# Block matching before a convolution stack: a pair of offsets in one subtraction and one square

## The chip, the core and the metric

The kernel runs on one core of a Trainium2 chip. The metric is the device time of one execution in microseconds. The profile comes from one profiled execution of the same program; "the span" is its time from first to last instruction. The engines are PE (TensorE, with its weight loads shown apart as PEld), DVE (VectorE), ACT (ScalarE), POOL (GpSimd) and SP (SyncE). Each runs its own list of instructions in order and waits on semaphores for the others.

## The reference

`x` is 8 images of 32 channels, 128 x 128, float32. It passes two layers, each with a group norm in front and a residual sum behind. The first layer begins with a block matching, and that is what the change is about:

```python
for dy in range(-SEARCH_R, SEARCH_R + 1):          # SEARCH_R = 2: 25 offsets
    for dx in range(-SEARCH_R, SEARCH_R + 1):
        yy = jnp.clip(jnp.arange(Hn) + dy, 0, Hn - 1)
        xx = jnp.clip(jnp.arange(Wn) + dx, 0, Wn - 1)
        sh = x[:, :, yy][:, :, :, xx]
        d = ((x - sh) ** 2).sum(1, keepdims=True)
        costs.append(_conv(d, ones, pad=PATCH // 2))   # 3x3 sum
...
_, idx = jax.lax.top_k(-jnp.transpose(cost, (0, 2, 3, 1)), K)   # K = 8
...
h = jax.nn.relu(_conv(_conv(xb, w1), w2, groups=CK, pad=1))
h = jax.nn.relu(_conv(_conv(h, w3), w4, groups=CK, pad=1))
wiener = jax.nn.sigmoid(_conv(_conv(h, w5), w6, groups=CK, pad=1))
filt = _conv(wiener * dct, inv_dct_w, groups=C)
```

For every pixel the 8 offsets of least cost are taken, the 8 shifted copies of the image are gathered into 256 channels (`xb`), and these pass three pointwise and three 3x3 depthwise convolutions and a filter. The second layer is a 5x5 convolution of each channel.

## The kernel before

**Layout of the block matching.** A normalised image stands in the tile `xn`: 128 partitions are 4 groups of rows by 32 channels, and each partition holds 38 rows of 132 columns (`HR`, `HX`): 32 rows of its own with 3 above and 3 below, and 128 columns with 2 of border on each side, filled with copies of the edge. A shift by an offset is then only another start address in the same tile. Since the squared difference for an offset and that for its opposite are the same numbers shifted, only 12 of the 25 offsets are computed (numbers 13 to 24; 12 is zero).

**Squares.** `prep(b)` (L364) normalises image `b` (L382, one operation on DVE) and then walks over 6 blocks of 6 rows (`SR`), and in each over 6 pairs of offsets: 36 pairs an image, 288 in all. A pair is one task, `squares` (L431), in three steps. On DVE, two subtractions (L442), one for each offset, of 6 rows and as many columns as the offset leaves: 132 for dx = 0, 131 for |dx| = 1, 130 for |dx| = 2, so 792, 786 or 780 elements a partition. On ACT, two squares (L450) in place. On PE, matmuls (L457) with a column of minus ones that add up the 32 channels and put each offset's cost in a row of its own of the PSUM tile `pd`; there are 2 by 2 of them in the code and 8 matmul instructions a pair in the trace. After the sixth pair `pd` is copied (L468) and sent to DRAM (L472), from where `costs` (L483) reads it back, sums 3x3 on DVE, transposes on PE and finds the 8 best with `max` and `max_index` (L534, L535). `places` (L540) turns these into addresses for the gather of the next image.

The difference tile `df` has the tag "df" and 4 buffers, each of 6 x 132 float32 a partition, so two pairs are in flight. A fifth subtraction waits for the matmuls that read the first.

**Order.** The instructions of PE, DVE and ACT stand in an order that the program writes out by hand. The main loop takes steps of 8 rows; in each step it goes through the three convolution stages of three different row blocks and the final filter of a fourth. Beside it run tasks in four queues: "D" (DVE work, run by `tick` for a credit, where a pair costs `PAIR` = 1.95 and at most two are taken in one round), "A" (ACT), "P" and "Q" (PE). A task gives up at each `yield` and is put into the queue that the yield names. In one stage of a step the order is about this: PE's pointwise matmuls for 128 of the 256 channels (L671) and their copies on ACT (L679); ACT's first tap of the depthwise convolution (L722); queue "P", then queue "Q" with the matmuls of the squares; a selector pass on ACT for the gather (L617, L618); `tick`, and with it the subtractions on DVE; the other eight taps of the depthwise convolution on DVE (L725, 8 x 1024 elements); pointwise matmuls for the other 128 channels (L695, copies L702); gather matmuls (L632, copy L639); queue "A" with the squares; the function of the previous depthwise stage (L729) on ACT; another selector pass; and the depthwise matmuls (L751, copies L764).

So on DVE the subtractions stand in front of the eight accumulates of L725, and on ACT the squares stand behind a selector pass and the copies, and in front of L729. The squares of image `b + 1` are computed while image `b` is convolved, mostly in the first two fifths of its time; those of image 0 come before everything else. One image takes some 812 us.

Of the kernel before, what the change touches and what calls it, by code (L numbers as in the profile page):

```python
# [8 lines left out]
F32 = mybir.dt.float32  # L9
BF16 = mybir.dt.bfloat16  # L10
U32 = mybir.dt.uint32
AF = mybir.ActivationFunctionType
# [3 lines left out]
P = 128  # L16
C, K, H, W = 32, 8, 128, 128
# [9 lines left out]
HX = W + 4  # L27
SR = 6
# [15 lines left out]
def bm3d_conv_preact(  # L44
# [16 lines left out]
    nc = tc.nc  # L61
# [5 lines left out]
    work = ctx.enter_context(tc.tile_pool(name="work", bufs=2))  # L67
# [142 lines left out]
    def push(task):  # L210
        want = next(task, None)
        if want:
            which, cost, *wait = want
            queues[which].append((cost, task, now[0] + (wait[0] if wait else 0)))
# [149 lines left out]
    def prep(b):  # L364
# [25 lines left out]
        for i in range((HR - 2) // SR):  # L390
            pd = ps_d.tile([P, SR // 2, HX], F32, name=f"pd_{b}_{i}", tag="pd")

            for aa in ((2, 4), (0, 0), (1, 1), (3, 2), (4, 3), (5, 5)):
                yield "D", PAIR
                push(squares(b, i, pd, xn, aa, sq, idx))
# [35 lines left out]
    def squares(b, i, pd, xn, aa, sq, idx):  # L431


        r0 = SR * i
        ds = []
        for e in range(2):
            o = 13 + 2 * aa[e] + e
            dy, dx = o // 5 - 2, o % 5 - 2

            ca, cz = max(0, -dx), min(HX, HX - dx)  # L440
            df = work.tile([P, SR, HX], F32, name=f"df_{b}_{i}_{o}", tag="df", bufs=4)
            nc.vector.tensor_sub(  # L442
                df[:, :, ca:cz],
                xn[:, r0 : r0 + SR, ca:cz],
                xn[:, r0 + dy : r0 + dy + SR, ca + dx : cz + dx],
            )
            ds.append((df, ca, cz))
        yield "A", 0
        for df, ca, cz in ds:
            nc.scalar.activation(df[:, :, ca:cz], df[:, :, ca:cz], AF.Square)  # L450
        yield "Q", 0

        for e in range(2):
            for h in range(2):
                df, ca, cz = ds[e]
                j = 2 * e + h
                nc.tensor.matmul(  # L457
                    pd[C * j : C * (j + 1), :, ca:cz],
                    neg[:, 28 - 4 * aa[e] : 60 - 4 * aa[e]],
                    df[:, SR // 2 * h : SR // 2 * (h + 1), ca:cz],  # L460
                    start=aa[0] == 2,
                    stop=aa[0] == 5,
                    skip_group_check=True,
                )
        if aa[0] < 5:
            return
        sm = work.tile([P, SR // 2, HX], F32, name=f"sm_{b}_{i}", tag="sm", bufs=1)
        nc.scalar.copy(sm, pd)  # L468
        for e in range(2):
            for h in range(2):  # L470
                j = 2 * e + h
                nc.gpsimd.dma_start(  # L472
                    sq[e::2, :, r0 + SR // 2 * h : r0 + SR // 2 * (h + 1)].rearrange(
                        "o g r x -> o g (r x)"
                    ),
                    sm[C * j : C * j + 24].rearrange("p r x -> p (r x)"),
                )

        q = {1: 0, 3: 1, 4: 2, 5: 3}.get(i)
        if q is not None:  # L480
            push(costs(b, q, sq, idx))
# [553 lines left out]
    with tc.manual_schedule(engines=ORDERED):  # L1035
# [19 lines left out]
        for s in range(len(steps) + 2):  # L1055
            if s < len(steps):
                b, n = steps[s]
# [120 lines left out]
```

## Time and profile before

Three runs: 6686.44, 6694.62 and 6697.99 us, median 6694.62. The profiled execution took 6691.29 us, with a span of 6689.5 us and a mean granted clock of 0.976.

| group | count | busy us | mean ns |
|---|---|---|---|
| DVE accumulate L725 | 3264 | 4032.5 | 1237 |
| PE depthwise matmuls L751 | 31680 | 2142.4 | 422 |
| ACT selector L617 | 1024 | 1170.9 | 1143 |
| ACT selector L618 | 1024 | 1086.1 | 1061 |
| PE matmuls of the squares L457 | 2304 | - | 518 to 534 |

Busy time is the time in which at least one instruction of the group ran; instructions of one engine overlap a little at their ends, so the busy time of a group is less than its count times the mean. "Idle before" is time in which the engine stood still just in front of an instruction, and the releaser is what ended that wait. The chain of waits is followed back from the last instruction; in this profile it reaches from 3509 us to the end.

Who waits in and around the squares, from the rows of their three lines: ACT for the subtractions 341.1 us in 87 waits (316.3 us in 70 waits after the first image's squares); DVE's subtractions for a free buffer 78.4 us in 18 waits; PE's matmuls for the squares 204.0 us in 255 waits (115.1 us in 168 after the first image's).

### The profile page before, as it was taken

The numbers are of one execution on the slowest core, as the hardware profiler recorded it, in microseconds if no ns is written. First come the engines' busy times: TensorE is split into PE (matmuls) and PEld (weight loads), VectorE is DVE, ScalarE is ACT, GpSimd is POOL, SyncE is SP. The second block draws the span as 40 slices with busy tenths as digits, with TensorE's granted clock in tenths as the row PEclk, the third lists the DMA queues.
The fourth block names the chain that finished last, engine by engine and source line by source line (L and its number), as shares of the span: only waits on it lengthen the run. The fifth ranks groups of instructions, "written<-read, shape, count | busy, mean of one in ns | idle before, by whom it ended". The sixth has DMA issues, their size and how long they took to land. (4 is left out here: it accounts for less than half of the span.)

```text
span 6689.5 us, 235037 instructions
## 1 busy us (share of the span) xinstructions
PE 6258.1 (94%) x102306; PEld 3229.6 (48%) x102306; DVE 5864.5 (88%) x8826; ACT 5055.3 (76%) x6698; POOL 3536.2 (53%) x5527
## 2 busy tenths in 40 slices
PE   4899899999999999999999999999999999999997
PEld 1444455544545445554454444544445454554553
DVE  7899988999889998899889988899988999877786
ACT  5787778777787777877787776877768777687772
POOL 8365447554475454754546544565446654445334
PEclk8899999999999999999999999999999999999998
DMA  4666666766566675666756657566665666566663
GB/s 95 150 153 153 151 151 151 173 153 158 150 165 157 159 161 137 162 162 156 172 138 164 161 142 168 144 167 158 152 154 151 167 155 154 142 170 163 154 155 80
DMA packets 811718, 1021.56 MB, mean 153 GB/s; under 512 B 257072, under 2 KB 622192, under 8 KB 810688
## 3 DMA queue, kind: packets, MB, share of 16 engines
q0 software_dynamic: 424608, 747.17, 43.9%
q1 hardware_dynamic: 383568, 258.11, 17.8%
q8 instruction: 805, 13.19, 0.8%
q10 hardware_dynamic: 2512, 1.25, 0.1%
q14 instruction: 225, 1.84, 0.1%
HBM read 554.82 MB, written 217.54 MB: 115 GB/s over the span
## 5 line engine op out<-in xcount | busy, mean ns | idle before, releaser
L725 DVE SCALAR_TENSOR_TENSOR acc<-tv,dwv,acc 128x1024 f32<-128x1024 f32 (+3 forms) x3264 | 4032.5, 1237 | 247.6 <-ACT acc L722 143.0
L751 PE MATMUL pw<-t,dwd 128*32 128x254 f32 (+7 forms) x31680 | 2142.4, 422 | 81.4 <-DMA t<-t 61.3
L603 POOL DMA_DIRECT2D ib<-idxd x1024 | 749.9, 733 | 1586.3 <-ACT sel L618 1311.6
L751 PEld LDWEIGHTS pw<-t,dwd 96*32 96x32 f32 (+1 forms) x31680 | 1090.4, 111 | 921.0 <-issue 445.7
L617 ACT ACTIVATE ib<-ib,nplace 128x1024 bf16<-128x1024 bf16 x1024 | 1170.9, 1143 | 49.5 <-DMA ib<-idxd 49.5
L618 ACT ACTIVATE sel<-ib 128x1024 f32<-128x1024 bf16 x1024 | 1086.1, 1061 | 32.5
L695 PE MATMUL p<-acc,lw 128*32 128x256 f32 x16768 | 1001.6, 383 | 23.7 <-ACT tv L679 23.0
L671 PE MATMUL pv<-acc,lw 128*32 128x512 f32 x8448 | 956.3, 590 | 46.5 <-DVE acc L818 39.8
L791 POOL DMA_DIRECT2D xf<-xbd x1088 | 651.3, 627 | 267.8 <-DMA out_dram<-xy 80.7
L695 PEld LDWEIGHTS p<-acc,lw 128*32 128x32 f32 x16768 | 575.0, 111 | 439.0 <-issue 82.5
L450 ACT ACTIVATE df<-df 128x786 f32<-128x786 f32 (+2 forms) x576 | 468.2, 861 | 343.7 <-DVE df L442 341.1
L679 ACT COPY tv<-pv 128x512 f32<-128x512 f32 (+2 forms) x784 | 437.5, 579 | 320.3 <-PE pv L671 309.4
L632 PE MATMUL pg<-sel,xt 120*32 120x88 f32 (+1 forms) x24576 | 616.0, 244 | 62.8 <-ACT sel L618 48.2
L632 PEld LDWEIGHTS pg<-sel,xt 120*32 120x32 f32 x24576 | 556.7, 111 | 235.6 <-ACT sel L618 71.0
L442 DVE TENSOR_TENSOR df<-xn 128x786 f32<-128x786 f32 (+2 forms) x576 | 531.7, 973 | 79.4 <-PE pd L457 78.4
L729 ACT ACTIVATE acc<-acc 128x1024 f32<-128x1024 f32 (+3 forms) x408 | 417.3, 1023 | 241.0 <-DVE acc L725 240.8
L764 ACT ACTIVATE acc<-pw 128x512 f32<-128x512 f32 (+2 forms) x808 | 438.7, 572 | 194.1 <-PE pw L751 192.9
L671 PEld LDWEIGHTS pv<-acc,lw 128*32 128x32 f32 x8448 | 281.4, 111 | 537.8 <-issue 435.2
L702 ACT COPY t<-p 128x512 f32<-128x512 f32 x800 | 424.3, 571 | 116.0 <-PE p L695 115.5
L722 ACT ACTIVATE acc<-tv,dwv 128x1024 f32<-128x1024 f32 (+3 forms) x408 | 455.1, 1115 | 36.5 <-PE pa L831 22.9
L671 PE MATMUL pv<-xb,lw 128*32 128x512 f32 x4096 | 470.9, 594 | 0.0
L695 PE MATMUL p<-xb,lw 128*32 128x256 f32 x8192 | 467.7, 379 | 0.0
(155 smaller groups left out, 5936.0 us busy)
## 6 DMA issues: line engine op xcount, KB each, us to landing
ib<-idxd POOLq DMA_DIRECT2D x1024, 256.0 KB, 4.6
xbd<-xb POOLq DMA_DIRECT2D x128, 1024.0 KB, 7.0
xf<-xbd POOLq DMA_DIRECT2D x960, 128.0 KB, 7.2
t<-t SPq DMA_DIRECT2D x792, 128.0 KB
t<-t SPq DMA_DIRECT2D x384, 256.0 KB
tv<-tv SPq DMA_DIRECT2D x384, 130.0 KB
xt<-xtd POOLq DMA_DIRECT2D x240, 180.0 KB, 4.6
xtd<-xl POOLq DMA_DIRECT2D x192, 96.0 KB, 3.1
```

The lines of the kernel that those rows point to most:

```text
L442: nc.vector.tensor_sub(df[:, :, ca:cz], xn[:, r0 : r0 + SR, ca:cz], xn[:, r0 + dy : r0 + dy + SR, ca + dx : cz + dx],)
L450: nc.scalar.activation(df[:, :, ca:cz], df[:, :, ca:cz], AF.Square)
L603: nc.gpsimd.dma_start(ib.rearrange("p g k y x -> p g (k y x)"), idxd[b][s4 % 8 // 2, s4 // 8 * 2 + s4 % 2, f] .rearrange("(g e k) x -> e g ...
L617: nc.scalar.activation(ib, ib, AF.Square, bias=nplace)
L618: nc.scalar.activation(sel, ib, AF.Relu, scale=-1.0, bias=1.0)
L632: nc.tensor.matmul(pg[C * j : C * (j + 1), :, :, xa:xz], xt[: 8 * QW, f * (NT // 2) + t], sels[j // 2][: 8 * QW, :, j % 2, :, xa:xz], star ...
L671: nc.tensor.matmul(ps[C * j : C * (j + 1), :hr], lhsT[:, g, P + C * j : P + C * (j + 1)], src(g)[:, h : h + hr], start=g == 0, stop=g == 1,)
L695: nc.tensor.matmul(ps[C * r : C * (r + 1), e, :nb], lhsT[:, g, s], rows[:, r : r + 4 * nb - 3 : 4], start=g == 0, stop=g == 1,)
L722: nc.scalar.activation(acc, rows, AF.Copy, scale=tap)
L725: nc.vector.scalar_tensor_tensor(acc, rows, tap, acc, op0=ALU.mult, op1=ALU.add)
L751: nc.tensor.matmul(pt[u][C * j : C * (j + 1), ka:kz, :nb, xa:xz], dwd[0:hi, i - 1, u, j, dx + 1], t[0:hi, j, ka:kz, :nb, xa + dx : xz + dx ...
L791: nc.gpsimd.dma_start(xf[p : p + C, m, j0:j1], src[g, m, (h + m + 1) % 2, :, :, ya:yz])
```

## The change

The two subtractions of a pair become one, over a tile with both differences, `[P, 2, 6, 132]`. The first operand is the image's own rows, read once for each offset (a broadcast dimension of size 2); the second is read by a hand-made access pattern whose extra dimension steps from one shifted start to the other. Both squares become one activation over the same tile. The tile has the pool's default of 2 buffers, each twice as large as before, so the memory is the same. Both offsets now use the same columns: 130 for every pair but that with dx = 0, which keeps 132 (the first in each block; it starts the sums in PSUM). The matmuls read their half of the tile and are as many as before. The order of tasks, `PAIR` and all else stay.

```diff
-        ds = []
-        for e in range(2):
-            o = 13 + 2 * aa[e] + e
-            dy, dx = o // 5 - 2, o % 5 - 2
-
-            ca, cz = max(0, -dx), min(HX, HX - dx)
-            df = work.tile([P, SR, HX], F32, name=f"df_{b}_{i}_{o}", tag="df", bufs=4)
-            nc.vector.tensor_sub(
-                df[:, :, ca:cz],
-                xn[:, r0 : r0 + SR, ca:cz],
-                xn[:, r0 + dy : r0 + dy + SR, ca + dx : cz + dx],
-            )
-            ds.append((df, ca, cz))
+        off = [divmod(13 + 2 * aa[e] + e, 5) for e in range(2)]
+        off = [(dy - 2, dx - 2) for dy, dx in off]
+        ca = min(min(2, 2 - dx) for dy, dx in off)
+        cz = max(max(2 + W, 2 + W - dx) for dy, dx in off)
+        if aa[0] == 2:
+            ca, cz = 0, HX
+        df = work.tile([P, 2, SR, HX], F32, name=f"df_{b}_{i}_{aa[0]}", tag="df")
+        own = xn[:, r0 : r0 + SR, ca:cz]
+        to = [HX * dy + dx for dy, dx in off]
+        other = bass.AP(
+            own.tensor,
+            own.offset + to[0],
+            [own.ap[0], [to[1] - to[0], 2], own.ap[1], own.ap[2]],
+        )
+        nc.vector.tensor_sub(
+            df[:, :, :, ca:cz],
+            own.unsqueeze(1).to_broadcast([P, 2, SR, cz - ca]),
+            other,
+        )
         yield "A", 0
-        for df, ca, cz in ds:
-            nc.scalar.activation(df[:, :, ca:cz], df[:, :, ca:cz], AF.Square)
+        nc.scalar.activation(df[:, :, :, ca:cz], df[:, :, :, ca:cz], AF.Square)
         yield "Q", 0
...
-                df, ca, cz = ds[e]
...
-                    df[:, SR // 2 * h : SR // 2 * (h + 1), ca:cz],
+                    df[:, e, SR // 2 * h : SR // 2 * (h + 1), ca:cz],
```

## The prediction

> **What bounds the kernel now.** I read the page first: the engine totals and the costliest groups.
>
> ```profile
> PE 6258.1 (94%) x102306; PEld 3229.6 (48%) x102306; DVE 5864.5 (88%) x8826; ACT 5055.3 (76%) x6698; POOL 3536.2 (53%) x5527
> ...
> L450 ACT ACTIVATE df<-df 128x786 f32<-128x786 f32 (+2 forms) x576 | 468.2, 861 | 343.7 <-DVE df L442 341.1
> ...
> L442 DVE TENSOR_TENSOR df<-xn 128x786 f32<-128x786 f32 (+2 forms) x576 | 531.7, 973 | 79.4 <-PE pd L457 78.4
> ```
>
> Three engines are close to full, so the average says little. The two groups that the change edits are 532 us of VectorE and 468 us of ScalarE. ScalarE stands idle 341 us in front of its squares, waiting for the subtractions. That wait is what I priced first. The windows of busy time over image 5 (one image is some 813 us) show that the limit changes hands:
>
> ```profile
> 4271.00:4340.00 69.00, 63.06 (x944) 34.38 (x948) 56.06 (x61) 65.54 (x90) 41.76 (x66) 0.98 0.52 130
> 4340.00:4720.00 380.00, 368.62 (x6008) 186.62 (x6004) 350.42 (x526) 300.96 (x394) 226.75 (x338) 0.99 0.67 164
> 4720.00:4800.00 80.00, 71.84 (x1139) 34.58 (x1134) 70.17 (x134) 54.99 (x74) 28.88 (x48) 0.96 0.51 130
> ```
>
> Columns after the length are busy us of PE, weight load, DVE, ACT and POOL, then clock and DMA. For 69 us ACT is the full one (65.5), then PE for 380 us (368.6). In the last stretch none is full: each waits for another. The chain of waits names the path there:
>
> ```profile
> 4284.43 3.00 ACT df L450 x4
> ...
> 4734.15 1.76 DVE df L442 x2
> 4735.91 0.02 issue
> 4735.93 0.86 ACT df L450
> 4736.79 0.95 ACT acc L729
> 4737.74 1.05 ACT ib L617
> ...
> 4741.84 1.17 ACT acc L722
> 4743.01 0.02 issue
> 4743.03 1.30 DVE acc L725
> ```
>
> The first line is one of four groups of four squares (4284, 4296, 4310, 4360) that stand on the chain while ACT is full: four steps of 0.75. The rest is a **crossing**: both subtractions, then only the last square (the first ran beside the second subtraction), then ACT's next work down to the copy L722 that lets VectorE go on. In image 5 the chain crosses so at 4271 (two pairs), 4734 and 4785. Between 4340 and 4690 it runs mostly over PE, and the squares are not on it.
>
> **The change part by part.**
>
> *Two subtractions become one.* Nearest rows, by shape: 968 ns for 128x780 and 1225 ns for the 128x1024 addition of L517, so 1.05 ns an element. One of 1560 elements takes 1225 + 536 x 1.05 = 1.79 us; one of 1584 takes 1.81. Today the two take 1.84 us from start to end (4734.06), 531.7/288 = 1.846 in the mean. So about 0.06 us a pair, 288 pairs: 17 us of VectorE busy time. No row shows a subtraction with a broadcast operand and three dimensions. L316 broadcasts both operands over two dimensions and takes 0.40 us for two of 64 elements, nothing unusual; I take no penalty. Bounds: nothing saved below, and at worst the slower of the two rates met on VectorE, the accumulate's 1284 ns for 1024 elements (1.25 an element), 1.95 us: 0.10 us lost a pair instead of 0.06 won.
>
> [...]
>
> *Two squares become one.* 861 ns for 786 elements and 1061 ns for 1024 (L729) give 0.84 ns an element, so 1061 + 536 x 0.84 = 1.51 us for 1560. Back to back, 1024 elements step by 0.95 on the chain and 786 by 0.75; 1560 then step by 1.40, against 1.50 for two. That is 0.10 us a pair, 29 us of ScalarE in all. On the chain it counts where ACT is full: four groups of two pairs an image, 0.8 us, and two single pairs at 4694 and 4704, 0.2 us.
>
> *The overlap that goes.* A square may now start only when both halves are subtracted. At 4734.06 the first square starts 0.98 us after the first subtraction and the squares end at 4736.79. Merged: 4734.06 + 1.79 + 0.01 + 1.51 = 4737.37, **0.58 us later**. With two pairs at 4271.32: the second merged subtraction starts at +1.72, ends at +3.51, its square at +5.03, so 4276.35 for 4275.86: 0.49 later. What waits behind on ACT is the function of the last depthwise (L729), two selector passes, PSUM copies and L722, and VectorE's next eight accumulates wait for that one.
>
> *The matmuls.* Four of a pair's eight used to run while the second square ran; now all eight follow. Eight take 0.66 us on the chain when they don't wait, so PE's end moves 0.33 more where PE waits for squares (168 waits, 115 us after the first image's start). Where PE has the pair ready long before, as from 4340 on, nothing moves. The price if that cover is gone: 0.33 us at each of about two places an image.
>
> *Buffers.* Four half tiles become two whole ones. A subtraction that waits for its buffer (18 waits, 78 us, up to 8.4) waits for eight matmuls instead of four: 0.33 us more, 6 us in all if every one were on the path. The chain holds no such wait, so I take nothing.
>
> *Columns.* 131 become 130 on five of twelve offsets. Matmuls of 393 and 390 elements are 519 and 518 ns; the whole is 1 to 2 us of busy time. Nothing. No DMA, no queue and no credit of the planner is touched, so the order of all else stays.
>
> **The sum.** Chain of one image: + 0.49 + 2 x 0.58 (crossings) - 0.8 - 0.2 (full ACT) - 0.06 (4755, subtractions followed by accumulates) = + 0.6 us. Seven images are prepared so: + 4 us. The first image's squares run before anything else: 14 pairs with ACT full (1.4 us won), 16 that are paced by VectorE (1.0 won), one crossing at the start: - 2. That makes + 2 us with the chain as it is. It can't stay quite as it is: by the waits ACT stands idle before 70 squares after the first image's start, ten an image, of which the chain uses three. At 1231.99, off the chain, VectorE then waited 1.00 us for L722, and would wait 1.58. I add one such place an image, 7 x 0.58 = 4 us. Together + 6 us.
>
> The profiled execution took 6691.29 us (span 6689.5), 3.3 us under the median of the runs, 6694.62. So 6697.3 on that scale and 6700.6 against the median; I forecast **6699**.
>
> **Rivals.**
>
> *The later squares decide (slower).* One mechanism: ACT's idle time before the squares means that ACT is the late one afterwards, so 0.58 us passes to VectorE or PE at each crossing. For it: the 1.00 us at 1240.96, and 3.67 us of PE idle behind the crossing of 4785. Against it: from 4340 to 4690 the chain is PE's. If nine crossings an image count, 9 x 0.58 - 1.06 = 4.2, x 7 = 29, less 2: + 27, about **6720**. From six crossings an image on it passes 0.2%.
>
> *VectorE decides (faster).* If its continuous stretches set the pace through most of an image and its work is simply shorter: - 17 us, and some of ACT's 29 where ACT is full, 5 to 7: about **6672**. For it: DVE is 88% busy overall, more than 92% between 4340 and 4720. Against it: in that stretch PE is 97% busy and the chain is PE's.
>
> *The merged instruction isn't shorter (slower).* With the accumulate's rate, 0.16 us a pair is lost against the plan and each crossing costs 0.74: 7 x (3 x 0.16 + 0.16) = + 4.5 on the chain, but 29 us of VectorE is added to an engine that has 12% idle; half of that on the path, over the forecast, gives **6718**.
>
> **How the numbers follow.** About what a measurement of this kernel can tell from no change is 0.2%, 13.4 us: 6681 to 6708. Forecast 0.58, later squares 0.27, VectorE decides 0.10, no shorter instruction 0.05. So faster 0.10, same 0.58, slower 0.32. The forecast's own range goes from all crossings hidden (7 x -1.06 - 2 = - 9, 6682) to five crossings an image (5 x 0.58 - 1.06 = 1.84, x 7, less 2: + 11, 6706 against the median). For 8 in 10 I take 6683 to 6721: it reaches the slower rivals and leaves out most of the faster one.
>
> **What would show it.** Right: 288 subtractions of 1.78 to 1.81 us and 288 squares of 1.50 to 1.53; the idle time of ACT before squares up from 341 us by 0.8 to 0.9 us a waiting pair; VectorE's idle before L725 for ACT's L722 (143 us) up; busy totals of DVE and ACT down by about 17 and 29 us. Wrong: subtractions longer than 1.85; an image's period (from one image's first subtraction to the next's, 812.5 us) that falls although ACT waits longer, which would say that the crossings have slack; or PE's waits for squares growing by more than 1 us each, which would put PE at the end of the crossing.

## The result and the profile after

The changed kernel takes 6717.02 us in the median of 17 runs (6704.78 to 6726.62), the kernel before 6695.23 us in the median of 17 (6675.38 to 6717.38). The ratio is **1.0028, with a 95% interval of 1.002 to 1.0037**: slower, by some 19 us. The profiled execution took 6717.02 us (span 6715.2, mean granted clock 0.969).

From the page of the changed kernel, the engine totals and the two groups that were edited (busy us, mean ns, then the idle time in front with its main releaser):

```profile
PE 6226.7 (93%) x102306; PEld 3211.0 (48%) x102306; DVE 5844.4 (87%) x8538; ACT 5022.4 (75%) x6410; POOL 3543.4 (53%) x5527
...
L455 ACT ACTIVATE df<-df 128x1560 f32<-128x1560 f32 (+1 forms) x288 | 431.1, 1518 | 400.2 <-DVE df L449 400.0
...
L449 DVE TENSOR_TENSOR df<-xn 128x1560 f32<-128x1560 f32 (+1 forms) x288 | 510.3, 1786 | 112.4 <-PE pd L461 100.1
```

Both edited engines do less: DVE 20 us less, ACT 33 us less. Yet ACT now stands idle 400.0 us in front of its squares (341.1 before), and DVE 100.1 us in front of its subtractions for a buffer (78.4 before). The kernel has less work and more waiting.

The chain of waits of the changed kernel shows one crossing with a single pair, in image 5 (start us, us, what):

```profile
4761.16 1.69 DVE df L449
...
4762.87 1.50 ACT df L455
4764.37 0.95 ACT acc L733
...
4769.42 1.16 ACT acc L726
...
4770.60 1.30 DVE acc L729
```

From the start of the subtraction to ACT's next work (L733, the old L729) it is 4764.37 - 4761.16 = 3.21 us. In the profile before, the crossing at 4734.15 went through two subtractions and only the last square: 4736.79 - 4734.15 = 2.64. The crossing is 0.57 us longer, and behind it stand the same selector pass, PSUM copies and L726 as before, and then VectorE's accumulates.

The waits by pair of engines (waiting instruction, releaser: us, times, longest) show where the waiting is. After:

```profile
ACT df L455 <- DVE df L449: 400.0, 116, 11.6
...
DVE acc L729 <- ACT acc L726: 149.4, 132, 5.3
...
PE pd L461 <- ACT df L455: 109.0, 90, 3.1
DVE df L449 <- PE pd L461: 100.1, 39, 9.7
```

and before:

```profile
DVE acc L725 <- ACT acc L722: 143.0, 133, 5.6
...
PE pd L457 <- ACT df L450: 42.0, 47, 3.6
```

The largest relative growth is PE's: its matmuls of the squares wait 109 us instead of 42. VectorE's wait for L726 grows too, but only by 6 us.

### The profile page after: what moved, and what is told of

The parts are those of the page before. It is cut to its first block, busy times and chain, and to the rows that moved or that the text cites. A ratio compares the mean times of both kernels' runs of the same rounds, so it can differ in the third digit from the quotient of the medians.

```text
span 6715.2 us, 234297 instructions
## 1 busy us (share of the span) xinstructions
PE 6226.7 (93%) x102306; PEld 3211.0 (48%) x102306; DVE 5844.4 (87%) x8538; ACT 5022.4 (75%) x6410; POOL 3543.4 (53%) x5527
## 4 chain that ended last, share of the span: by engine, by line
PE 41%; DVE 29%; ACT 10%; DMA 9%; POOL 6%; issue 5%; SPq 0%; ACTq 0%; POOLq 0%; DVEq 0%
DVE acc L729 19%; PE pw L755 14%; PE pv L675 10%; PE p L699 9%; DMA t<-t 3%; PE pg L636 3%; POOL xtd L422 2%; DVE df L449 2%; DVE idx L539 2%; ACT ib L621 2%; ACT df L455 2%; PE pc L814 2%; DMA xf<-xbd 1%; DVE acc L822 1%; ACT acc L726 1%
## 5 line engine op out<-in xcount | busy, mean ns | idle before, releaser
L729 DVE SCALAR_TENSOR_TENSOR acc<-tv,dwv,acc 128x1024 f32<-128x1024 f32 (+3 forms) x3264 | 4032.2, 1237 | 254.5 <-ACT acc L726 149.4
L755 PE MATMUL pw<-t,dwd 96*32 96x254 f32 (+7 forms) x31680 | 2137.7, 422 | 79.7 <-DMA t<-t 62.0
L455 ACT ACTIVATE df<-df 128x1560 f32<-128x1560 f32 (+1 forms) x288 | 431.1, 1518 | 400.2 <-DVE df L449 400.0
L449 DVE TENSOR_TENSOR df<-xn 128x1560 f32<-128x1560 f32 (+1 forms) x288 | 510.3, 1786 | 112.4 <-PE pd L461 100.1
L733 ACT ACTIVATE acc<-acc 128x1024 f32<-128x1024 f32 (+3 forms) x408 | 417.2, 1023 | 241.7 <-DVE acc L729 241.6
L726 ACT ACTIVATE acc<-tv,dwv 128x1024 f32<-128x1024 f32 (+3 forms) x408 | 455.1, 1115 | 36.9 <-PE pa L835 23.9
```

What stands on the lines that cost most here:

```text
L449: nc.vector.tensor_sub(df[:, :, :, ca:cz], own.unsqueeze(1).to_broadcast([P, 2, SR, cz - ca]), other,)
L455: nc.scalar.activation(df[:, :, :, ca:cz], df[:, :, :, ca:cz], AF.Square)
L726: nc.scalar.activation(acc, rows, AF.Copy, scale=tap)
L729: nc.vector.scalar_tensor_tensor(acc, rows, tap, acc, op0=ALU.mult, op1=ALU.add)
L755: nc.tensor.matmul(pt[u][C * j : C * (j + 1), ka:kz, :nb, xa:xz], dwd[0:hi, i - 1, u, j, dx + 1], t[0:hi, j, ka:kz, :nb, xa + dx : xz + dx ...
```

## The experiments

All of them keep the computation whole. Where a pair is "split", it has two subtractions and two squares in the changed kernel's tile of both differences, with its 2 buffers and its columns. The edits are shown without branches that are never taken. Each ratio is against the kernel before, run on the same chip.

**The overlap alone.** The kernel before, with a pair's two squares in reverse order. Nothing is merged and nothing is saved, but the first square to be issued now needs the later subtraction:

```diff
-        for df, ca, cz in ds:
+        for df, ca, cz in ds[::-1]:
             nc.scalar.activation(df[:, :, ca:cz], df[:, :, ca:cz], AF.Square)
```

> The kernel before with the two squares of a pair in the other order: the one of the second subtraction first. Nothing is merged or saved; the first square now waits for both subtractions and the matmuls, whose first four read the other half, wait for both squares. If the lost overlap of the halves is the cause: squares end 0.75 us later at a place where ScalarE waits for the subtractions, and the kernel is as slow as the changed one or slower, ratio 1.002 to 1.006, with ScalarE's idle time before squares up from 341 us by some 60 and PE's before the matmuls up from 204 us to about 290. If the buffers' release by whole pairs or the long instructions themselves are the cause: ratio 0.999 to 1.001.

Ratio **1.0058 (1.0043 to 1.0074)**. One crossing of this kernel on its chain of waits:

```profile
4777.11 1.76 DVE df L442 x2
...
4778.89 1.60 ACT df L450 x2
4780.49 0.95 ACT acc L729
```

Both squares stand behind both subtractions: 4780.49 - 4777.11 = 3.38 us instead of 2.64. Its waits are those of the changed kernel: ACT 397.8 us in 113 waits before squares, VectorE 107.3 us in 43 for buffers. So the loss of the overlap is enough to make the kernel slower, without any merged instruction. The change loses less than this. Its crossing is shorter and its two engines have less to do, which would explain it; no run separates the two.

**The tile without the merging.** Every pair split:

```diff
-        nc.vector.tensor_sub(
-            df[:, :, :, ca:cz],
-            own.unsqueeze(1).to_broadcast([P, 2, SR, cz - ca]),
-            other,
-        )
+        for e in range(2):
+            s = own.offset + to[e]
+            nc.vector.tensor_sub(
+                df[:, e, :, ca:cz],
+                own,
+                bass.AP(own.tensor, s, [own.ap[0], own.ap[1], own.ap[2]]),
+            )
         yield "A", 0
-        nc.scalar.activation(df[:, :, :, ca:cz], df[:, :, :, ca:cz], AF.Square)
+        for e in range(2):
+            nc.scalar.activation(df[:, e, :, ca:cz], df[:, e, :, ca:cz], AF.Square)
```

> The changed kernel's tile of a whole pair, its two buffers and its 130 columns, but two subtractions and two squares, one for each half. If the release of a buffer by whole pairs is the cause: VectorE's waits for matmuls in the first image go from 0.8 us to about 10 as in the changed kernel, and the ratio is 1.002 to 1.003. If the lost overlap is the cause: ratio 0.999 to 1.001, waits before squares and matmuls as before (341 and 204 us), and the waits for buffers up by no more than 6 us.

Ratio 0.9994 (0.9984 to 1.0003), no difference that can be told. Buffers that come free by whole pairs and the 130 columns cost nothing by themselves; VectorE stands idle 88.5 us before its subtractions, 71.1 of them put down to the matmuls (79.4 and 78.4 before). The page of this kernel:

```profile
L466 ACT ACTIVATE df<-df 128x780 f32<-128x780 f32 (+1 forms) x576 | 468.1, 859 | 338.7 <-DVE df L452 336.0
```

336.0 us of idle time before the squares is the value before the change.

**Each merge alone.** One subtraction with two squares, and two subtractions with one square:

```diff
         nc.vector.tensor_sub(
             df[:, :, :, ca:cz],
...
-        nc.scalar.activation(df[:, :, :, ca:cz], df[:, :, :, ca:cz], AF.Square)
+        for e in range(2):
+            nc.scalar.activation(df[:, e, :, ca:cz], df[:, e, :, ca:cz], AF.Square)
```

> One subtraction for both halves, but two squares. Lost overlap: the first square starts 0.81 us later, the squares end 1.79 + 0.01 + 1.61 = 3.41 us after the subtraction's start instead of 2.73, so 0.68 later, and nothing is saved on ScalarE; the first four matmuls still run beside the second square. Ratio 1.002 to 1.004. If only the long square is to blame (because the matmuls wait for it): 0.999 to 1.001.

```diff
-        nc.vector.tensor_sub(
...
+        for e in range(2):
+            s = own.offset + to[e]
+            nc.vector.tensor_sub(
...
         nc.scalar.activation(df[:, :, :, ca:cz], df[:, :, :, ca:cz], AF.Square)
```

> Two subtractions, but one square over both halves. Lost overlap: the square ends 1.85 + 0.01 + 1.51 = 3.37 us after the first subtraction's start instead of 2.73, 0.64 later, ScalarE's 0.10 us a pair are saved, and all eight matmuls follow the square. Ratio 1.001 to 1.004, near the changed kernel's 1.0028. If only the subtraction is to blame: 0.998 to 1.000, from ScalarE's saving.

Ratios 1.0036 (1.0023 to 1.005) and 1.0034 (1.0022 to 1.0045). Either merge alone takes the whole overlap: with one subtraction neither square can start early, with one square the first half waits for the second. Both have the idle time of ACT before squares at 392 to 393 us. The crossings on the chains of the five kernels, beside their ratios:

| kernel | crossing, us | ratio |
|---|---|---|
| before | 2.64 | 1 |
| after | 3.21 | 1.0028 |
| two subtractions, one square | 3.28 | 1.0034 |
| one subtraction, two squares | 3.32 | 1.0036 |
| squares in reverse order | 3.38 | 1.0058 |

Each value is that of one crossing with a single pair; others of the same kernel lie up to 0.05 us higher, so the two middle kernels can't be told apart by it. The order of the ratios is that of the crossings, though neighbours' intervals overlap, and the last kernel also saves nothing on its engines.

**First image or later ones.** The first image's squares run alone; those of the other seven run beside a convolution. With a condition on the image (`b`), one part of the pairs is split:

```diff
+        if b == 0:
+            for e in range(2):
...
+        else:
             nc.vector.tensor_sub(
```

> The changed kernel, but the first image's pairs, whose squares run before all else, in two subtractions and two squares. In the profiles the second image's squares start 5.3 us later in the changed kernel than before, counted from the first subtraction. If that part of the loss is the first image's own: this start is back at 352 us after the first subtraction (357 in the changed kernel) and the ratio falls from 1.0028 to about 1.002. If the loss is made in the seven other images alone and the start only shifts work: 1.0028 stays.

Ratio 1.0037 (1.0022 to 1.0051) in 6 runs, which overlaps the changed kernel's interval. In this profile the second image's first subtraction came 351.8 us after the first image's, as in the kernel before, against 357.1 after the change; but 5 us of 6700 is within the width of that interval, so the run left the share of the first image open. The same kernel once more, in more rounds, beside its counterpart, which splits the seven others (`b > 0`):

> The counterpart, once more and in more rounds: only the first image's pairs are split, those of images 1 to 7 stay merged. If the later images hold most of the loss, the ratio is 1.002 to 1.003 (1.0028 less at most 0.0008); if the first image holds most of it, near 1.0. The two kernels' excess over 1 should add up to the changed kernel's 0.0028 if the shares are independent.

> The changed kernel with the pairs of images 1 to 7 split again into two subtractions and two squares; only the first image's 36 pairs stay merged. In the profile the second image's first subtraction should come 357 us after the first image's, as in the changed kernel (351.8 where the first image is split). If the later images' crossings hold most of the loss, the ratio is the all-split one, 0.9994, plus at most 5.3 us of 6700: 0.999 to 1.001. If the first image holds most of it, the ratio is near the changed kernel's: 1.002 to 1.003.

| split | ratio | ACT idle before squares, later images | PE idle before matmuls for squares, later images |
|---|---|---|---|
| all, as before the change | 1 | 316.3 us, 70 waits | 18.5 us, 27 waits |
| first image | 1.0021 (1.001 to 1.0032) | 364.9 us, 92 waits | 63.0 us, 59 waits |
| later images | 0.9998 (0.9987 to 1.001) | 315.1 us, 70 waits | 21.6 us, 27 waits |
| none, the change | 1.0028 (1.002 to 1.0037) | 365.9 us, 92 waits | 67.7 us, 60 waits |

The first row is the kernel before itself. The two excesses, 0.0021 and -0.0002, add up to 0.0019, with the change's 0.0028 inside their joint uncertainty. The later images hold most of the loss, and the waits switch with their pairs and with nothing else. What was expected of the second image's start came true in one only of the two: 355.7 us with the first image merged, but 356.3 this time with it split, where the clock granted from 200 to 380 us was 0.94 instead of 0.97. The other profiles of this document agree better: 351.7 to 352.5 us in the six with the first image split, 354.5 to 357.1 us in the four with it merged whole. So merging the first image delays the second by some 2 to 5 us; that this is still there at the end no ratio shows.

**Merging where nobody waits.** Split but for 22 pairs in each later image, those at whose places ACT hardly waits (18.0 us in 12 waits in this profile):

```diff
+        k = 6 * i + ((2, 4), (0, 0), (1, 1), (3, 2), (4, 3), (5, 5)).index(aa)
+        full = b and (2 <= k < 16 or k in (17, 19, 21, 23, 25, 27, 29, 31))
+        if not full:
...
```

> One subtraction and one square only for the 22 pairs an image (images 2 to 8) in front of which ScalarE does not wait for VectorE; two of each for the other 14 and for all of the first image. Lost overlap: no square ends later where an engine waits for it, ScalarE saves 0.10 us a pair in the stretch in which it is full, 4 groups of two pairs an image on the chain, so 0.8 x 7 = 6 us at most: ratio 0.9985 to 1.0003, with ScalarE's idle time before squares near 341 us. If a long instruction costs wherever it stands: 1.001 to 1.002.

Ratio 1.0002 (0.9991 to 1.0012). 154 of the 288 pairs are merged at no loss that can be told, so the loss of the change sits mostly in the remaining pairs, those in front of which ACT waits. No gain is seen either, though the 6 us that were expected at most lie at the edge of the interval. PE's matmuls wait 32.1 us for the squares of the later images here, against 18.5 before the change: PE waits some 14 us more here without a loss that can be told.

**Squares a round later.** The changed kernel, with the squares one round of the queue after their subtraction, and in the main loop at most one pair a round:

```diff
+    most = [2]
...
-                    if at <= now[0] and (c != PAIR or pairs[0] < 2)
+                    if at <= now[0] and (c != PAIR or pairs[0] < most[0])
...
-        yield "A", 0
+        yield "A", 0, 1 if b else 0
...
+        most[0] = 1
         for s in range(len(steps) + 2):
```

> The changed kernel with one pair a round at most in the main loop, and the squares of images 2 to 8 issued one round after their subtraction, so that ScalarE hardly ever waits for a subtraction. Lost overlap, taken to its end: with the subtraction long done the squares are on no path, ScalarE's 316 us of idle time before squares (70 waits) go below 100, and the crossings of the chain (three an image, 2.6 to 4.5 us each) are gone: ratio 0.993 to 0.999. If ScalarE's idle time only moves to its next wait, for VectorE's accumulates: 0.999 to 1.002. If one pair a round makes the next image's addresses late, PE waits at the start of an image: above 1.002.

Ratio **0.996 (0.9945 to 0.9974)**: faster than both kernels. Its page:

```profile
L456 ACT ACTIVATE df<-df 128x1560 f32<-128x1560 f32 (+1 forms) x288 | 437.9, 1521 | 33.9 <-DVE df L450 33.8
```

The 400 us have become 33.8, all of it in the first image. Its waits:

```profile
ACT acc L734 <- DVE acc L730: 373.4, 141, 8.8
...
DVE df L450 <- PE pd L462: 198.3, 41, 12.4
...
DVE acc L730 <- ACT acc L727: 85.0, 72, 5.0
```

ACT's idle time is not gone; 132 us of it stand now before L734, where it waits for accumulates (373.4 us, against 241.6 after the change). But VectorE waits 85.0 us for ACT's L727 instead of 149.4: a square that has just been subtracted no longer stands in front of that copy. The price is a longer wait of VectorE for buffers (198.3 us), since a pair's tile is held a round longer. All this is read from one profile of each kernel.

One pair a round could have done this by itself. So it was tried with the squares in the same round, without the one changed `yield`:

> As round_later with one pair a round at most in the main loop, but with the squares in the round of their subtraction, as in the changed kernel. If the gain of round_later comes from the squares' place: ratio 1.002 to 1.004, near the changed kernel's 1.0028, and ScalarE's idle time before squares about 400 us. If it comes from one pair a round: 0.996 to 0.998.

Ratio 1.0143 (1.0127 to 1.0159), with ACT idle before squares 522.6 us in 137 waits. This is outside both expectations: one pair a round alone is the slowest of all. ACT stands before the squares 21 times more than after the change; whether that is the whole of the loss was not followed. So the gain comes from the delay of the squares and not from one pair a round. The delay with two pairs a round was not run.

**In that order, split or merged.** With the crossing off the path, does merging pay? All pairs split, and only the first image's split:

> As round_later (one pair a round, squares of images 2 to 8 one round after their subtraction), but with two subtractions and two squares. If the later squares alone bring the gain: ratio 0.996 to 0.998, as round_later's 0.996 or a little more for the 17 us of VectorE and 29 us of ScalarE that are not saved. If the merged instructions bring it once the squares are off the path: 0.999 to 1.001.

> As round_later, but the first image's pairs in two subtractions and two squares. The second image's squares start 352 us after the first subtraction instead of 355 and the ratio is 0.0005 under round_later's 0.996 if the first image's loss stays to the end, 0.996 if it is made up later.

Ratios 0.9941 (0.9928 to 0.9955) and **0.9927 (0.9914 to 0.9941)**. The second is the fastest version found: 6657.18 us, against 6705.3 of the kernel before on the same chip. It merges the pairs of the later images and splits the first image's. The two intervals overlap, so a gain from merging there is likely at best and not shown. Both ratios are below what was expected (0.996 to 0.998, and 0.996 or 0.0005 less). The 0.996 was measured on another chip, beside its own runs of the kernel before; between it and 0.9927 lie some 22 us, and the first image's delay of 2 to 5 us does not account for them. Why is open.

## Why the prediction was right or wrong

The likeliest case (no measurable difference, 6699) did not come. The measured 6717 lies near the 6720 of the rival that was given 0.27, **the later squares decide**, and within the range of 6683 to 6721, which had been drawn wide enough to reach that rival. The rival's mechanism is what the runs show; its nine crossings an image are not, so that its number came so close is partly luck.

*Right: the price of the instructions.* The groups by shape of the changed kernel:

```profile
L449 DVE TENSOR_TENSOR df<-xn 128x1560 f32<-128x1560 f32 x240 | 424.7, 1780 | 77.5 <-PE pd L461 65.5 <-ACT df L455 6.4 <-ACT acc L768 5.6
...
L449 DVE TENSOR_TENSOR df<-xn 128x1584 f32<-128x1584 f32 x48 | 87.1, 1814 | 34.9 <-PE pd L461 34.7
...
L455 ACT ACTIVATE df<-df 128x1560 f32<-128x1560 f32 x240 | 360.0, 1514 | 315.6 <-DVE df L449 315.4
```

1.780, 1.814 and 1.514 us (1.79, 1.81 and 1.51 expected). The group of subtractions fell by 531.7 - 510.3 = 21.4 us, 0.07 us a pair (0.06 expected). DVE lost 20 us (17 expected) and ACT 33 us (29). In the trace before, eight subtractions in a row at 1023.10 us span 7.18 us, a step of 0.88 us where one takes 0.97 to 0.99: the next one starts before the last has ended, which left little to save between two of them. The rival of an instruction that isn't shorter falls, and with it "VectorE decides": the work did get shorter and the time did not.

*Right: the price of a crossing.* + 0.58 us, measured + 0.57; and ACT's L726 as the wait that hands it to VectorE. Summed over a run, this wait is 133.5 to 143.0 us (136.8 in the mean) in the four kernels that keep the overlap where ACT waits, and 141.2 to 159.7 us (150.0) in the six that lose it at the later images.

That the lost overlap at these places, and not something else of the change, carries the time is shown by the reversed squares (slower with nothing merged), by the split pairs (no difference with all the rest of the change in place) and by the 22 pairs an image that are merged at no cost where ACT hardly waits.

*Wrong: the sum.* + 6 us was forecast and some + 19 came. Three terms are in question, and the runs do not divide the missing 13 us among them.

The first is "I add one such place an image, 7 x 0.58 = 4 us", four crossings an image in all. By the formula of the rival, 7 x (n x 0.58 - 1.06) - 2, the + 19 us would ask for n = 7 if nothing else were wrong. But the changed kernel's chain of waits, which reaches over the whole run, has 31 crossings (places where a subtraction is followed by its square) in the seven images, three to five in each. These are their subtractions in image 5, the others of the chain left out:

```profile
4298.69 3.51 DVE df L449 x2
...
4606.62 1.70 DVE df L449
...
4729.58 1.69 DVE df L449
...
4761.16 1.69 DVE df L449
...
4812.25 1.71 DVE df L449
```

The chain of the kernel with only the first image merged, counted in the same way, has 24. So the count was off by little: 31 crossings at 0.57 us make 17.7 us at most, since one that was not on the path before had some slack.

The second is what the sum took off: "- 0.8 - 0.2 (full ACT)" an image, 7 us in all, and "- 2" for the first image. On the chain of image 5 the four groups of squares did become shorter as forecast, 2.80 to 2.82 us instead of 2.99 to 3.08, but no run shows that either saving reaches the end. Merging the 22 pairs an image gave 1.0002, merging the first image alone 0.9998, and there the profiles have a delay where the sum had a gain. Without these two terms the crossings alone would come near the 19 us; that is an argument, and no run shows it.

The third is the matmuls. "0.33 us at each of about two places an image", 7 x 2 x 0.33 = 5 us, was worked out and then did not enter the sum, without a reason. PE's matmuls of later images did wait longer, 67.7 us after for 18.5 before. But the growth by "more than 1 us each", the sign of a PE that ends the crossing, did not come: from 27 waits of 0.7 us it went to 60 of 1.1. Nor is most of this growth needed for the loss. With one subtraction and two squares, where half of the matmuls can still run beside the second square, PE waits only 35.7 us in 35 waits, and the ratio is 1.0036. A place where PE does wait, in the timeline of the changed kernel (start, us, instruction, idle before):

```profile
4812.16 1.77 DVE L449 TENSOR_TENSOR df<-xn 128x1560 f32<-128x1560 f32 x1
...
4813.97 1.51 ACT L455 ACTIVATE df<-df 128x1560 f32<-128x1560 f32 x1 [11.52 <-DVE df L449]
...
4815.53 1.53 PE L461 MATMUL pd<-df,neg 128*32 128x390 f32 x8 [2.73 <-ACT df L455]
...
4820.05 6.02 PE L699 MATMUL p<-acc,lw 128*32 128x256 f32 x64 [2.99 <-ACT tv L683]
...
4820.52 1.15 ACT L726 ACTIVATE acc<-tv,dwv 128x1024 f32<-128x1024 f32 x1
```

ACT had been idle 11.5 us, PE then waits 2.73 us for the square, and again 2.99 us for a copy of ACT, whose work stands behind that square.

*Wrong: the buffers.* "I take nothing", with 6 us as the most. The waits grew by 100.1 - 78.4 = 21.7 us, in the first image from 0.7 to 10.4 us. There the timeline of VectorE before shows subtractions back to back:

```profile
46.88 6.27 DVE L442 TENSOR_TENSOR df<-xn 128x792 f32<-128x792 f32 x7
```

and after, waits between them:

```profile
53.50 3.48 DVE L449 TENSOR_TENSOR df<-xn 128x1560 f32<-128x1560 f32 x2 [1.80 <-PE pd L461]
```

Subtraction, square and matmuls of a pair now follow each other whole, and with two buffers that round trip paces VectorE. The two large buffers are not at fault: with them and split pairs these first-image waits were 2.3 us, and with the four small buffers and reversed squares 9.3 us.

*Open.* Where the 19 us lie image by image can't be read from single executions: in two of the same kernel (only the first image split) image 5 took 824.0 and 816.7 us from its first subtraction to the next image's. How much slack the crossings had that came onto the chain was not followed.

## What to carry to other kernels

Before two halves of a producer are merged, look at what the consumer does in front of them: if it stands waiting, the first half's work ran beside the second half's, and merging puts it behind, at every such place (0.57 us later here). Count the consumer's waits as the most places that may pay (here ten an image, of which three to five stood on the chain after the change), and set the price of one against what the merge saves on the path, which may be nothing. Where the consumer waits at all, moving it a round later, with other work between, was worth more here (0.4 to 0.7%) than the saved instructions, whose gain by themselves no run could show.

## What the runs showed of the hardware

The granted clock of PE differed between kernels whose work on PE had shifted only a little. From 85 to 150 us the first image's squares end and little else runs on PE. There the clock was 0.82 before the change, 0.53 after it, and 0.79 with all pairs split, for nearly the same matmuls (192 to 194) in 33.37, 30.40 and 35.54 us of busy time. Shorter windows show where the difference lies (from:to, length, busy us of PE, weight load, DVE, ACT and POOL, granted clock, DMA share, GB/s). Before:

```profile
105.00:125.00 20.00, 8.92 (x42) 1.59 (x42) 18.02 (x54) 8.47 (x12) 19.03 (x32) 1.00 0.28 62
```

and after:

```profile
84.00:87.00 3.00, 0.00 (x0) 0.00 (x0) 2.93 (x3) 0.00 (x0) 3.00 (x6) 1.00 0.27 73
87.00:105.00 18.00, 8.25 (x40) 2.24 (x40) 17.08 (x57) 8.75 (x9) 18.00 (x23) 0.51 0.50 119
105.00:125.00 20.00, 9.94 (x54) 1.70 (x58) 17.86 (x60) 9.82 (x10) 18.36 (x29) 0.50 0.31 76
```

Between 105 and 125 us PE works in rounds of some 3.4 us, with gaps of 1.1 to 1.7 us before and 1.8 to 2.5 us after. Here is one round of each, before and after:

```profile
108.31 1.74 PE L457 MATMUL pd<-df,neg 128*32 128x390 f32 x8 [1.61 <-ACT df L450]
```

```profile
113.45 1.53 PE L461 MATMUL pd<-df,neg 128*32 128x390 f32 x8 [1.76 <-ACT df L455]
```

In the changed kernel PE had stood idle for 3.67 us until 87.60. From there on the clock stayed at half (0.51 and 0.50), although no gap up to 125 us was longer than 2.63 us, while the kernel before held the full clock (1.00) through its rounds from 105 to 125 us. And earlier in the changed kernel, from 74 to 83 us, the clock was 0.50 too, where since 61 us no gap had been longer than 1.1 us until one of 2.03 at 80.9. So the length of the gap in front does not by itself account for the clock here. PE's gaps in a round differ between the two kernels, but no run varied them alone. The clock is not the cause of the loss: the kernel with only the first image merged had 0.50 from 85 to 150 us and no measurable loss, one subtraction with two squares had the mean clock of the kernel before (0.974 to 0.975 in the median run) and lost 0.36%, and the squares a round later had a mean clock of 0.967 and were faster.
